# Sparse products by halves of 64 rows on TensorE's column halves, with the gathers of y for eight blocks moved into step 1

## The chip, the cores and the metric

The kernel runs on one core of one Trainium2 chip. A core has a matrix engine (TensorE, in the profile PE, its weight loads PEld), a vector engine (DVE), an activation engine (ACT), a general engine (GpSimd, POOL) and a queue engine that issues most transfers (SyncE, SP). The metric is the time of one execution in microseconds on the device. The kernel before has a median of 1310.05 us over 11 runs (1305.77 to 1312.8).

## The reference

A graph of N = 2708 nodes has features x of 256 columns and a matrix adj (2708 x 2708) in which about 0.3% of the entries are not zero. Two layers follow each other; the second has two steps.

```
x1 = layernorm(x + relu(concat(x, adj @ x) @ weight + bias))     # layer 0
R  = (adj + I) / row sums of (adj + I)                           # layer 1
Xf = Xa = x1;  Z = 0
for n in 0, 1:
    A  = top_p_attention(Xa, W1, W2, W3)   # softmax of q k^T, per row the largest up to 0.9, renormalised
    Xf = R @ Xf
    Xa = A @ Xa
    Z += Xf @ U1[n].T + Xa @ U2[n].T
out = layernorm(x1 + layernorm(x1 + Z) * g + b)
```

Everything is float32. R is as sparse as adj, A is dense before the cut and is computed in full.

## The kernel before, in words

Rows come in NB = 22 blocks of 128, the last of 20 rows (EDGE). D = 256. Products by U1 and U2 are made before those with R and A, so that R is applied to two arrays of 256 columns: yf (s = 0), and v (s = 1), which is v + R yf as it comes out of s = 0. Both lie in DRAM as yf_d and v_d, of which a row of 1 KB belongs to a node.

- **Stage 0 and stage 1** (to 285 us): x @ weight, and then for each block m the dense product of adj, read as 704 KB in two loads, with layer 0's norm. While adj's block lies in SBUF, DVE notes which of its columns hold anything (name_columns, L287).
- **Lists.** An output block has 128 rows, and so few entries that no more than 7 x 128 = 896 of the 2708 columns hold one. Lists (L297) makes a list of these columns for each block: DVE takes the largest eight of each segment again and again (take), up to CAP = 160 a segment; end joins the seven segments of a block into one list, by way of DRAM, with seven scatters of POOL. ix holds the list as CC = 7 columns of 128 indices. Blocks 0 to 15 make one list tile, joined at the end of stage 1, and blocks 16 to 21 another, whose rounds lie in step 1's first nine periods and which is joined at t = 8.
- **Step 1** (349 to 725 us): the loop over t = 0 to 21 with six slots g each: transposes and products of A's block t (turn, products: L527, L564), the logits of t + 3 (L507), the exponentials of t + 2 on ACT, the largest and their sum on DVE. In slot (m - 2, 3) adj_gather(m) has POOL fetch the listed rows of adj's block, transposed in DRAM: 7 indirect transfers of 128 rows of 512 bytes (L367) and one addition of the identity (L369). Four and five slots later adj_store writes them to adjc_d. In (20, 2) and (20, 5) POOL gathers y of blocks 0 and 1 (L719).
- **The border.** ya_pair (L662) projects two blocks of step 1's result by U2 into ya, the tile that step 2's products read; ACT copies each pair (L675, L678). Its tile is otherwise free in step 1. Behind the copies ACT has the exponentials and the search of step 2's first blocks (L966, L969), in the order of its queue.
- **Step 2** (786 us on): 24 periods (per) of six slots. A period has the transposes of block per - 2, its products with ya, the logits and exponentials of block per + 2, a search for the cut on ACT (try_act) and on DVE, and r_units(n): n of R's products, L749. A block has CC + 1 = 8 of them: 7 with gathered columns, one for the block's own 128 columns (own_d), all of them 128 x 128 by 128 x 256 in one accumulator. `units` says how many a period has: 16 ahead of the loop, 8 in periods 0 and 1, 18 in each of periods 2 to 9 (the rest of s = 0), none in 10, 16 in each of 11 to 21 (s = 1).
- **y's ring.** yg has room for two blocks. As r_units begins a block, it loads the next: adj's rows come from adjc_d (SyncE), y's by 7 indirect transfers of POOL (y_load), in both s. s = 1's first load waits until the last v is stored (r_out, `m == NB - 1`). From period 13 on the finals (two norms, out) come with each period; their four additions on POOL stand among the gathers.

The order on each engine is that of the program: the loops write it down, and each engine takes its own instructions one after the other. POOL's indirect transfers are issued by POOL itself, so whatever POOL waits for holds back all behind it; a plain transfer waits in SyncE's queue in the same way.

Of the kernel before, what the change touches and what calls it, by code (L numbers as in the profile page):

```python
# [38 lines left out]
CAP = 160  # L39
ML = 16  # L40
CW, CC = 128, 7
# [11 lines left out]
def gnn_two_layer_kernel(ctx: ExitStack, tc: tile.TileContext, N, xT_d, x_d, adj_d, w0_d, b0_d,  # L53
# [31 lines left out]
    assert NB == 3 * KS + 1 and CW == P and CAP % 8 == 0 and N < NB * P  # L85
# [16 lines left out]
    c.part_d = dram.tile([NB, KS, CAP + 1], FP, name="part_d")  # L102
    c.list_ds = [dram.tile([b - a, KS * CAP], I32, name="list_d") for a, b in ((0, ML), (ML, NB))]
    c.adjc_d = dram.tile([NB, CW, CC * P], FP, name="adjc_d")
    c.yf_d = dram.tile([P, NB, D], FP, name="yf_d")
    c.v_d = dram.tile([P, NB, D], FP, name="v_d")
    c.own_d = dram.tile([NB, P, P], FP, name="own_d")
# [12 lines left out]
    NF = 6 * NB + 4  # L120
# [28 lines left out]
def fast_path(ctx, tc, c, flags, fint, xT_d, x_d, w0_d, b0_d, w1_d, w2_d, w3_d, u1_d, u2_d, g_d, b_d):  # L149
# [43 lines left out]
    xT = big.tile([P, DC, N], FP, tag="Y", name="xT")  # L193
# [73 lines left out]
    names = room[:, :NB * (NB - 1)].rearrange("p (m c) -> p m c", c=NB - 1)  # L267
    at = NB * (NB - 1)
    ramp = room[:, at:at + NB]
    some = room[:, at + NB:at + 2 * NB]  # L270
    LROOM = 3 * P + 2 * CAP + 1 + KS * (CAP + 1)
    first_room = room[:, at + 2 * NB:at + 2 * NB + LROOM]
# [6 lines left out]
    ix = small.tile([P, NB, CC], I32, tag="ix", name="ix", bufs=1)  # L279
    nc.gpsimd.iota(ix.rearrange("p m c -> p (m c)"), pattern=[[0, NB * CC]], base=LAST, channel_multiplier=0)  # L280
    for i, (a, b) in enumerate(((0, ML), (ML, NB))):
        nc.gpsimd.dma_start(out=c.list_ds[i][:, :CW * CC].rearrange("m (p c) -> p m c", c=CC), in_=ix[:, a:b, :])
    before_m = small.tile([NB, 1], FP, tag="before_m", name="before_m", bufs=1)
# [3 lines left out]
    def name_columns(m):  # L287
        for h in range(2):
            nc.vector.tensor_reduce(some[:, h * KH:(h + 1) * KH], adj_of[m][h], AX.X, ALU.max,
                                    apply_absolute_value=True)  # L290
        nc.vector.tensor_scalar(some, some, 0.0, None, op0=ALU.not_equal)
        for a, b, o in ((0, m, 0), (m + 1, NB, -1)):
            if a < b:
                nc.vector.scalar_tensor_tensor(names[:, m, a + o:b + o], ramp[:, a:b], -float(m * P * NB),
                                               some[:, a:b], op0=ALU.add, op1=ALU.mult)

    class Lists:  # L297


        def __init__(self, a, b, flag, room):  # L300
            self.a, self.b, self.n, self.flag = a, b, KS * (b - a), flag
# [22 lines left out]
        def end(self):  # L324
# [9 lines left out]
            nc.gpsimd.dma_start(out=c.part_d[a:b].rearrange("m s k -> (m s) k"), in_=self.out[:n])  # L334
            nc.gpsimd.dma_start(out=self.all, in_=c.part_d[a:b])
            run = small.tile([NB, KS], FP, tag="run", name="run", bufs=1)[:b - a]
            to = small.tile([NB, KS], I32, tag="to", name="to", bufs=2)[:b - a]
# [4 lines left out]
            list_d = c.list_ds[a > 0]  # L342
# [5 lines left out]
            nc.gpsimd.dma_start(out=ix[:CW, a:b, :], in_=list_d[:, :CW * CC].rearrange("m (p c) -> p m c", c=CC))  # L348

    adj_rows = adj_d.rearrange("m p k i -> (m p k) i")  # L350
    staged = {}

    to_turn = []

    def name_y():
        while to_turn:
            m = to_turn.pop()
            nc.gpsimd.tensor_scalar(ix[:CW, m, :], ix[:CW, m, :], m * P * NB, P * NB - 1, op0=ALU.subtract, op1=ALU.min)

    def adj_gather(m):  # L360
# [4 lines left out]
        name_y()  # L365
        for i in range(CC):
            nc.gpsimd.indirect_dma_start(out=a[:CW, i, :], out_offset=None, in_=adj_rows,  # L367
                                         in_offset=bass.IndirectOffsetOnAxis(ap=ix[:CW, m, i:i + 1], axis=0))
        nc.gpsimd.tensor_tensor(a[:p, CC, :], a[:p, CC, :], ident[:p], op=ALU.add)  # L369
        to_turn.append(m)  # L370
        staged[m] = a

    def adj_store(m, h):

        i = (CC + 1) // 2
        if h == 0:
            nc.sync.dma_start(out=c.adjc_d[m, :, :i * P], in_=staged[m][:CW, :i, :].rearrange("p c i -> p (c i)"))
            return
        a = staged.pop(m)
        nc.sync.dma_start(out=c.adjc_d[m, :, i * P:], in_=a[:CW, i:CC, :].rearrange("p c i -> p (c i)"))  # L380
        nc.sync.dma_start(out=c.own_d[m, :rows(m), :], in_=a[:rows(m), CC, :])
# [64 lines left out]
    lists = Lists(0, ML, flags[:, NF - 4:NF - 2], first_room)  # L446
    for m in range(NB):
# [18 lines left out]
        if m == ML:  # L466
            lists.turn()
# [15 lines left out]
        if m >= ML:  # L483
            i = m - ML
            lists.take(CAP // 8 * i // (NB - ML), CAP // 8 * (i + 1) // (NB - ML))
    assert not weights
    lists.end()
    y_room = big.tile([P, DC * N], FP, tag="Y", name="yg")
    YW = 2 * (CC + 1) * D
    yg = y_room[:, :YW].rearrange("p (s c d) -> p s c d", s=2, d=D)  # L490
    spares = [y_room[:, YW + D * i:YW + D * (i + 1)] for i in range(4)]
    lists = Lists(ML, NB, flags[:, NF - 2:], yg[:, 1].rearrange("p c d -> p (c d)"))
# [218 lines left out]
    arrived, loads, held = {}, {}, {}  # L711
    later = [[], []]
    ready = []

    def y_load(s, m):
        y = yg[:, m % 2]
        rows_d = (c.yf_d, c.v_d)[s].rearrange("p k d -> (p k) d")
        for i in range(CC):
            nc.gpsimd.indirect_dma_start(out=y[:CW, i, :], out_offset=None, in_=rows_d,  # L719
# [177 lines left out]
    for t in range(NB):  # L897
# [6 lines left out]
        for g in range(NG):  # L904
# [16 lines left out]
            if g == 2:  # L921
                if t + 3 < NB:
                    extract1(t + 3)
                if t < 9:
                    lists.take(2 * t + 2, 2 * t + 4)
# [805 lines left out]
```

## Time and profile before

| | |
|---|---|
| median of 11 runs | 1310.05 us (1305.77 to 1312.8) |
| profiled execution | 1310.61 us, span 1308.7 us, mean granted clock 0.979 |
| stage 1, one block | 11.03 us (28 to 271 us in all) |
| step 1, one period | 17.54 us (t loop 349 to 725 us) |
| ya, then ACT's start of step 2 | 725 to 752 us, 752 to 786 us |
| step 2, periods 2 to 8 | 24.16 us each |
| step 2, periods with v and finals (15 to 20) | 25.2 us each |
| one product of R (two records) | 0.433 us |
| one gather by POOL | 0.95 us and 0.30 to the next |

The page gives each engine's busy time, the chain of work that ended last (followed back from the last instruction, each piece to what released it), and groups of instructions by line. In float32 one product is two records on PE. A period's time is read as the distance between the first transposes (L527) of two periods in the chain. The time of an execution is its span and about 2 us around it.

### The profile page before, as it was taken

The page shows a single profiled execution, that of the slowest core. Times are in us where ns is not written, and L with a number is a line of the kernel's source. Part 1 is how long each engine was busy: PE and PEld are TensorE (multiplying, and loading weights), DVE is VectorE, ACT ScalarE, POOL GpSimd, SP SyncE. Part 2 cuts the span into 40 slices and gives each one's busy share as a digit, 9 for nine tenths or more (in the row PEclk, how much of TensorE's full clock was granted, in tenths as well). Part 3 has the DMA queues.
Part 4 walks back from the last instruction along what each step waited for, and adds up shares of the span by engine and source line. Part 5 has one row for each costly group of instructions (what it writes and reads, how often), then busy time and mean ns, then how long its engine had stood idle before and what let it go on. Part 6 is the DMA issues. An engine that isn't in the chain of part 4 may idle for free.

```text
span 1308.7 us, 18883 instructions
## 1 busy us (share of the span) xinstructions
PE 1235.3 (94%) x5764; PEld 892.6 (68%) x5764; DVE 996.3 (76%) x3406; ACT 735.1 (56%) x1337; POOL 635.5 (49%) x594
## 2 busy tenths in 40 slices
PE   8999999979899999999999969999998999999985
PEld 6878877843477777777766647777765776666763
DVE  2445554874999997977761389889889899999996
ACT  2000111025555666656555497888878889989931
POOL 1000000003475442677755077788756768888850
PEclk9999999989999999999999989999998999999997
DMA  7465444523322220233223155656644545655541
GB/s 193 151 189 169 155 141 158 165 67 123 113 73 86 69 69 10 60 95 95 81 74 100 50 161 165 191 166 189 196 105 144 170 131 162 191 157 152 173 106 38
DMA packets 101993, 166.27 MB, mean 127 GB/s; under 512 B 17394, under 2 KB 74358, under 8 KB 101882
## 3 DMA queue, kind: packets, MB, share of 16 engines
q1 hardware_dynamic: 75596, 108.91, 26.1%
q0 software_dynamic: 20544, 51.17, 14.9%
q10 hardware_dynamic: 5742, 4.89, 1.4%
q8 instruction: 48, 0.79, 0.3%
q14 instruction: 63, 0.52, 0.1%
HBM read 130.87 MB, written 34.03 MB: 126 GB/s over the span
## 4 chain that ended last, share of the span: by engine, by line
PE 75%; ACT 16%; DVE 5%; issue 2%; DMA 1%; SPq 0%; ACTq 0%; DVEq 0%
PE acc L564 26%; PE acc L257 16%; PE lg L507 9%; PE misc L749 7%; PE tr L527 6%; ACT e L969 3%; ACT e L844 3%; ACT e L966 3%; PE acc L651 2%; ACT wT L530 2%; PE acc L462 2%; PE misc L426 2%; ACT e L848 2%; PE acc L672 2%; PE misc L699 2%
## 5 line engine op out<-in xcount | busy, mean ns | idle before, releaser
L530 ACT COPY wT<-tr 128x512 f32<-128x512 f32 (+2 forms) x258 | 131.8, 518 | 225.1 <-PE tr L527 223.4
L564 PE MATMUL acc<-ya,wT 128*128 128x256 f32 (+1 forms) x924 | 233.9, 393 | 12.5 <-ACT wT L530 12.1
L564 PE MATMUL acc<-x,wT 128*128 128x256 f32 (+1 forms) x924 | 230.5, 388 | 0.0
L719 POOL DMA_INDIRECT yg<-v_d,ix x154 | 193.4, 1256 | 65.8 <-issue 25.6
L564 PEld LDWEIGHTS acc<-ya,wT 128*128 128x128 f32 (+1 forms) x924 | 170.4, 193 | 67.2 <-ACT wT L530 24.3
L564 PEld LDWEIGHTS acc<-x,wT 128*128 128x128 f32 (+1 forms) x924 | 165.2, 189 | 71.0 <-issue 37.4
L719 POOL DMA_INDIRECT yg<-yf_d,ix x154 | 189.3, 1229 | 48.3 <-issue 24.3
L257 PE MATMUL acc<-y,adj_t 128*128 128x257 f32 (+1 forms) x924 | 208.4, 382 | 0.0
L257 PEld LDWEIGHTS acc<-y,adj_t 128*128 128x128 f32 (+1 forms) x924 | 171.8, 189 | 32.7 <-issue 8.9
L367 POOL DMA_INDIRECT adj_t<-in_adj,ix x154 | 167.6, 1088 | 51.5 <-issue 44.0
L749 PE MATMUL misc<-yg,adj_t 128*128 128x256 f32 (+1 forms) x704 | 180.2, 391 | 5.7 <-DMA yg<-yf_d,ix 4.2
L507 PE MATMUL lg<-k,q 64*128 64x512 f32 (+3 forms) x528 | 150.1, 596 | 19.5 <-ACT e L848 12.3
L749 PEld LDWEIGHTS misc<-yg,adj_t 128*128 128x128 f32 (+1 forms) x704 | 125.0, 190 | 53.6 <-issue 22.6
L527 PE MATMUL tr<-ident,e 128*128 128x128 f32 (+2 forms) x946 | 147.4, 275 | 2.3 <-DVE e L1088 2.3
L527 PEld LDWEIGHTS tr<-ident,e 128*128 128x128 f32 (+2 forms) x946 | 113.8, 139 | 41.3 <-issue 18.0
L334 POOL DMA_DIRECT2D part_d<-e x1 | 0.6, 573 | 287.3 <-DVE e L333 287.3
L966 ACT ACTIVATE e<-e,st 128x2708 f32<-128x2708 f32 (+1 forms) x43 | 113.5, 2640 | 0.1
L439 ACT COPY x1T<-tr 128x256 f32<-128x256 f32 (+1 forms) x22 | 8.0, 364 | 186.6 <-PE tr L438 186.6
L969 ACT ACTIVATE e<-e,st 128x2708 f32<-128x2708 f32 (+1 forms) x42 | 110.9, 2642 | 0.1
L570 DVE MAX8 cand<-e 128x8 f32<-128x170 f32 (+1 forms) x352 | 87.2, 318 | 26.8 <-ACT e L514 26.8
L1030 DVE MAX8 cand<-w 128x8 f32<-128x136 f32 (+1 forms) x440 | 106.8, 289 | 0.0
L507 PEld LDWEIGHTS lg<-k,q 64*128 64x128 f32 (+1 forms) x528 | 38.9, 181 | 52.9 <-issue 21.4
(237 smaller groups left out, 1764.6 us busy)
## 6 DMA issues: line engine op xcount, KB each, us to landing
adj_t<-in_adj SPq DMA_DIRECT2D x44, 704.0 KB
adj_t<-adjc_d SPq DMA_DIRECT2D x44, 448.0 KB
adjc_d<-adj_t SPq DMA_DIRECT2D x22, 256.0 KB
base<-za_d SPq DMA_DIRECT2D x41, 128.0 KB
adjc_d<-adj_t SPq DMA_DIRECT2D x22, 192.0 KB
xt<-in_x ACTq DMA_DIRECT2D x21, 128.0 KB
x_d<-x SPq DMA_DIRECT2D x21, 128.0 KB
x1b_d<-xb SPq DMA_DIRECT2D x21, 128.0 KB
```

The source lines that it names most:

```text
L257: nc.tensor.matmul(acc[:p, :n], lhsT=halves[k // KH][:kw, k % KH, :p], rhs=y[:kw, k, :n], start=k == 0, stop=stop and k == NB - 1)
L367: nc.gpsimd.indirect_dma_start(out=a[:CW, i, :], out_offset=None, in_=adj_rows, in_offset=bass.IndirectOffsetOnAxis(ap=ix[:CW, m, i:i + 1] ...
L507: nc.tensor.matmul(lg[:p, h, :b - a], lhsT=q[o, t * P:t * P + p], rhs=keys[s][o, i, :b - a], start=True, stop=True)
L527: nc.tensor.transpose(tr[:kw, k % 4, :p], e[:p, k * P:k * P + kw], ident[:p, :p])
L530: nc.scalar.copy(wT[:, :full, :p], tr[:, :full, :p])
L564: nc.tensor.matmul(acc[:p, :D], lhsT=wT[:kw, k % 4, :p], rhs=y[:kw, k, :], start=k == 0, stop=k == NB - 1)
L570: nc.vector.max(dst[:p, i * 8:(i + 1) * 8], src[:p, i * step:i * step + w])
L719: nc.gpsimd.indirect_dma_start(out=y[:CW, i, :], out_offset=None, in_=rows_d, in_offset=bass.IndirectOffsetOnAxis(ap=ix[:CW, m, i:i + 1], ...
L749: nc.tensor.matmul(acc[:p, :D], lhsT=a[:kw, k, :p], rhs=y[:kw, k, :], start=k == 0, stop=k == CC)
L966: nc.scalar.activation(scr[:b.p, :N], e, AF.Relu, bias=b.nz, scale=b.l[k], accum_out=b.relu)
L969: nc.scalar.activation(scr[:b.p, :N], e, AF.Sign, bias=b.nz, scale=b.l[k], accum_out=b.sign)
L1030: nc.vector.max(b.cand[:p, 8 * i:8 * i + 8], low[:p, SEG2 * i:SEG2 * (i + 1)])
```

## The change

- **Lists by halves.** Every block of 128 rows becomes two halves of HP = 64 rows with a list of its own: CC = 4 columns of 128 indices for each half (NQ = 8 for a block), CAP = 96. An entry of adj_rows is now 64 elements, 256 bytes. ixa, a second index tile, holds the indices of adj's halves, and ix those of y; both are made once per join (columns) rather than per block (name_y goes).
- **Three joins.** Blocks 0 to 8 are joined in stage 1 (m = 19), 9 to 17 in the prologue of step 1, 18 to 21 in step 1 at t = 7, g = 2.
- **The gathers.** adj_gather has 8 transfers (4 for the edge block) for 7; adj_store follows 8 and 9 slots later rather than 4 and 5. y_load has 8 for 7.
- **The products.** For each k of 4, two products of 64 columns of weights stand one after the other, the one on PSUM rows 0 to 63 and the other on rows 64 to 127; then the own product as before. A unit of r_units is a pair or the own product, 5 a block for 8.
- **y ahead.** For blocks 6, 8, ..., 20 and s = 0, POOL gathers y in step 1, in slot (m - 1, 4), into one of two stages that lie in ya's tile (ya[0:8] and ya[8:16]); SyncE stores them nine slots later to yg_d, 1 MB each, and step 2 loads them from there with one transfer of SyncE.
- **The units.** 10 ahead of the loop, 5 in periods 0 and 1, 90 over periods 2 to 8, 5 in the second half of period 9, 105 over periods 10 to 21.

```diff
-CAP = 160
-ML = 16
-CW, CC = 128, 7
+CAP = 96
+LISTS = ((0, 9), (9, 18), (18, 22))
+HP = 64
+AHEAD = tuple(range(6, 22, 2))
+CW, CC = 128, 4
+NQ = 2 * CC
...
+            lists.turn()
+        if m == LISTS[1][1]:
+            first, lists = lists, Lists(1, rooms[1])
             lists.turn()
...
+        if m == LISTS[1][1]:
+            first.end(nc.gpsimd)
+            first.gather(nc.gpsimd)
+        if m == LISTS[1][1] + 1:
+            first.join(nc.gpsimd)
+            first.columns()
...
+        def columns(self):
+            a, b = self.a, self.b
+            for g in range(2):
+                nc.gpsimd.tensor_scalar(ixa[:CW, a + g:b:2, :], ix[:CW, a + g:b:2, :], 2, g, op0=ALU.mult, op1=ALU.add)
+            for m in range(a // 2, b // 2):
+                own = ix[:CW, 2 * m:2 * m + 2, :]
+                nc.gpsimd.tensor_scalar(own, own, m * P * NB, P * NB - 1, op0=ALU.subtract, op1=ALU.min)
...
+    def parts(m):
+        return [(k, g, 2 * k + g) for k in range(CC) for g in range(2 if rows(m) > HP else 1)]
...
+        flat = a.rearrange("p k i -> p (k i)")
+        for k, g, i in parts(m):
+            nc.gpsimd.indirect_dma_start(out=flat[:CW, HP * i:HP * (i + 1)], out_offset=None, in_=adj_rows,
+                                         in_offset=bass.IndirectOffsetOnAxis(ap=ixa[:CW, 2 * m + g, k:k + 1], axis=0))
         nc.gpsimd.tensor_tensor(a[:p, CC, :], a[:p, CC, :], ident[:p], op=ALU.add)
-        to_turn.append(m)
         staged[m] = a
...
+    def y_gather(s, m, y):
+        rows_d = (c.yf_d, c.v_d)[s].rearrange("p k d -> (p k) d")
+        for k, g, i in parts(m):
+            nc.gpsimd.indirect_dma_start(out=y[:CW, i, :], out_offset=None, in_=rows_d,
+                                         in_offset=bass.IndirectOffsetOnAxis(ap=ix[:CW, 2 * m + g, k:k + 1], axis=0))
+
+    def y_stage(m):
+        k = NQ * (AHEAD.index(m) % 2)
+        return ya[:, k:k + NQ, :]
+
+    def y_store(m):
+        nc.sync.dma_start(out=c.yg_d[AHEAD.index(m)], in_=y_stage(m)[:CW].rearrange("p c d -> p (c d)"))
+
     def y_load(s, m):
         y = yg[:, m % 2]
-        rows_d = (c.yf_d, c.v_d)[s].rearrange("p k d -> (p k) d")
-        for i in range(CC):
-            nc.gpsimd.indirect_dma_start(out=y[:CW, i, :], out_offset=None, in_=rows_d,
-                                         in_offset=bass.IndirectOffsetOnAxis(ap=ix[:CW, m, i:i + 1], axis=0))
+        if s == 0 and m in AHEAD:
+            nc.sync.dma_start(out=y[:CW, :NQ, :].rearrange("p c d -> p (c d)"), in_=c.yg_d[AHEAD.index(m)])
+        else:
+            y_gather(s, m, y)
         y_in[s, m] = y
...
-            kw = CW if k < CC else p
-            nc.tensor.matmul(acc[:p, :D], lhsT=a[:kw, k, :p], rhs=y[:kw, k, :], start=k == 0, stop=k == CC)
+            if k < CC:
+                flat = a.rearrange("p k i -> p (k i)")
+                for g in range(2 if p > HP else 1):
+                    w, i = min(p, HP), 2 * k + g
+                    nc.tensor.matmul(acc[HP * g:HP * g + w, :D], lhsT=flat[:CW, HP * i:HP * i + w],
+                                     rhs=y[:CW, i, :], start=k == 0, stop=False)
+            else:
+                nc.tensor.matmul(acc[:p, :D], lhsT=a[:p, CC, :p], rhs=y[:p, NQ, :], start=False, stop=True)
...
+    second.join(nc.gpsimd)
+    second.columns()
...
+    y_ahead = {(m - 1, 4): m for m in AHEAD}
+    y_stores = []
...
-                if t < 9:
-                    lists.take(2 * t + 2, 2 * t + 4)
-                if t == 8:
-                    lists.end()
+                if t < ROUNDS // 2:
+                    lists.take(2 * t, 2 * t + 2)
+                if t == ROUNDS // 2:
+                    lists.end(nc.sync)
+                if t == ROUNDS // 2 + 1:
+                    lists.join(nc.gpsimd)
+                    lists.columns()
+            if (t, g) == (ROUNDS // 2, 5):
+                lists.gather(nc.sync)
             if (t, g) in at:
                 adj_gather(at[t, g])
-                stores += [(NG * t + g + i, at[t, g], i - 4) for i in (4, 5)]
+                stores += [(NG * t + g + 8 + i, at[t, g], i) for i in (0, 1)]
+            if y_stores and y_stores[0][0] <= NG * t + g:
+                y_store(y_stores.pop(0)[1])
+            if (t, g) in y_ahead:
+                m = y_ahead[t, g]
+                y_gather(0, m, y_stage(m))
+                y_stores.append((NG * t + g + 9, m))
...
+    TURN = 9
     units = {0: CC + 1, 1: CC + 1}
     rest = each - first - sum(units.values())
-    units.update({p: rest * (p - 1) // 8 - rest * (p - 2) // 8 for p in range(2, 10)})
-    units.update({p: each * (p - 10) // 11 - each * (p - 11) // 11 for p in range(11, 22)})
+    units.update({p: rest * (p - 1) // (TURN - 2) - rest * (p - 2) // (TURN - 2) for p in range(2, TURN)})
+    units[TURN] = CC + 1
+    rest = each - units[TURN]
+    units.update({p: rest * (p - TURN) // (21 - TURN) - rest * (p - TURN - 1) // (21 - TURN)
+                  for p in range(TURN + 1, 22)})
+
+    def r_share(per, g):
+        late = NG // 2 if per == TURN else 0
+        upto = [units.get(per, 0) * max(0, i - late) // (NG - late) for i in (g, g + 1)]
+        return upto[1] - upto[0]
```

## The prediction

> **What bounds the kernel now.** I read the page's shares, then its chain, then the chain piece by piece through one step-2 period, then windows of one period of each stage, then POOL's and ACT's timelines around the border between step 1 and step 2.
>
> The busy line of PE and the chain:
>
> ```profile
> PE 1235.3 (94%) x5764; PEld 892.6 (68%) x5764; DVE 996.3 (76%) x3406; ACT 735.1 (56%) x1337; POOL 635.5 (49%) x594
> ...
> PE 75%; ACT 16%; DVE 5%; issue 2%; DMA 1%; SPq 0%; ACTq 0%; DVEq 0%
> ```
>
> The chain has PE for 75%, but R's products (L749) are only 7% of it though their group has 180.2 us: most lie beside something else. The second resource is ACT. Windows of one period of step 1, of step 2 with R's first products (s=0), without R, and with R's second products and finals (s=1); the columns are PE, PEld, DVE, ACT, POOL, clock, DMA:
>
> ```profile
> 593.00:610.60 17.60, 17.60 (x90) 12.70 (x88) 13.84 (x54) 10.62 (x21) 12.46 (x13) 1.00 0.34 102
> 841.32:865.50 24.18, 23.87 (x117) 17.99 (x115) 18.71 (x65) 19.93 (x34) 19.38 (x16) 1.00 0.62 180
> 980.90:1004.20 23.30, 19.01 (x79) 12.75 (x78) 20.58 (x77) 19.92 (x33) 13.96 (x13) 0.89 0.43 131
> 1136.30:1161.50 25.20, 23.80 (x112) 16.98 (x111) 23.59 (x86) 22.30 (x40) 20.85 (x19) 1.00 0.56 168
> ```
>
> Step 1 is PE alone. An s=0 period is PE (23.87 of 24.18). The period without R shows what is left without it: ACT's loop. An s=1 period is ACT, with POOL close behind. The chain inside an s=0 period, with PE's work by length:
>
> ```profile
> 936.88 1.13 PE lg L507 x4
> 938.01 1.92 PE acc L564 x8
> 939.93 0.44 PE tr L527 x4
> 940.37 1.30 PE misc L749 x6
> 941.67 1.73 PE acc L564 x8
> ```
>
> A product of R is two of these records: 1.30/3 = 0.433 us. L564's eight records take 1.73 us, but 1.92 behind L507, whose records use half of TensorE's rows: leaving a partial mode costs 0.19.
>
> **The products on column halves.** Before: 44 blocks of 8 products = 3.46 us each. After: 4 pairs of 64-column halves and one full product. How far do a pair's halves overlap? The edge block's last products (L550) stand on four column groups in turn. The chain has them at
>
> ```profile
> 1290.34 3.30 PE acc L550 x44
> ```
>
> that is 75 ns a record where a full one takes 217; the last four run alone (0.86 us), so forty take 2.4 us, 61 ns each, 3.6 of 4 groups at once. I take a pair of halves at the price of one product, 0.433 (bounds: 0.433 and 0.866). But each run of pairs between full-width work changes the mode twice. The edge block's own R products, 20 columns wide, show that (the chain again, 974 us is the neighbour):
>
> ```profile
> 973.01 1.40 PE misc L749 x6
> 974.41 1.92 PE acc L564 x8
> ```
>
> 1.40 for 1.30 and 1.92 for 1.73: 0.10 to enter, 0.19 to leave, 0.3 a run. No skipping it: r_units interleaves two or three units with every transpose and product group.
>
> s=0, periods 2 to 8 (first transposes 788.25 to 957.36, 24.16 each). Before 18 products, 7.79 us. After 90 units over 7 periods, 12.86 each: 10.29 pairs and 2.57 full products, 5.57 us, and about 6.3 runs by 0.3, 1.9 us: 7.46. Some runs follow L507, whose exit is paid anyway (two by 0.1). PE's load falls 0.3 to 0.5. ACT's floor under it: from a period's first transposes to ACT's last wT copy 20.4 us without finals (981.04 to 1001.4), then L564 1.92, and what R has in slot 0: two units and a mode change, 1.2: 23.5. So I take a period of 23.65, a gain of 0.5, and **-3.5** for seven (bounds 0 and -5.5, the latter ACT's floor with two units at no mode price).
>
> The skill has a sterner price. The Trainium skill, "TensorE: Matmul & The Clock Gate", section "Measured speedup vs the span model", gives three column tiles 2.38 times the throughput of one, not 3. No pair of 64 columns runs in this trace, so neither is excluded; by that efficiency a pair would cost some 0.55 us (an estimate), the period 24.7, and this term would be about +3 in place of -3.5.
>
> s=1 and its neighbours. Period 9 now has 5 units in its second half instead of 18: it waits for the first gathers of v, which stand behind the last product of s=0, +1.2 (0 to +3). Period 10 had no units and yet 24.97 us from its first transposes to the next, 1.9 over the following 23.1-23.3, because period 11's first product waited for v; that wait falls into period 9: -1.75. Periods 10 to 21 have 8.75 units for 16; PE is not their bound, ACT's slot 0 carries 1 unit with a mode change (0.73) for 2 (0.87): -0.14 each, and POOL (14 gathers by 1.25 = 17.5, stalls 4.6, four adds by 0.73 = 25.0 of 25.2) allows hardly more. Together **-2** (bounds +2 and -5).
>
> **POOL in step 1.** This is where the change adds most. POOL's timeline of before at the border:
>
> ```profile
> 709.48 0.95 POOL L719 DMA_INDIRECT yg<-yf_d,ix  x1 [0.30 <-issue]
> 710.73 0.95 POOL L719 DMA_INDIRECT yg<-yf_d,ix  x1 [0.30 <-issue]
> 711.98 0.95 POOL L719 DMA_INDIRECT yg<-yf_d,ix  x1 [0.30 <-issue]
> 751.69 0.11 POOL L957 MEMSET e<- 128x12 f32 x1 [38.77 <-PE acc L672]
> ```
>
> A gather takes 1.25 us, whatever the size of its rows (512 bytes of adj at 1.25, 1 KB of y at 1.25): halving adj's rows halves nothing. POOL now ends 39 us before step 2. After: third list joined one period earlier, so free about 505-514 (before 531.8; the seven scatters take 508.3 to 530.8). Until y of block 20 stand 100 gathers of adj and 56 of y: 156 by 1.25 = 195 us, 13 additions of 0.47 = 6, and the stalls: while DVE runs L635 (3.03 us) a gather takes 3.0-3.2, 2.0 to 2.6 more, once a period, 20 to 30 in all. Sum 726 to 746, I take 740. Then it lands (3.3) and SyncE stores 1 MB (3.4 to 5.8 us at the 308 to 180 GB/s of the windows, with 2 or 3 to land): 749.
>
> Who waits: the stage is ya itself, 16 of 22 blocks' room. ya_pair's copy of blocks 8 and 9 overwrites block 20's stage. ACT's timeline of before has that copy, the end of ya, and the exponentials behind it:
>
> ```profile
> 737.38 0.59 ACT L675 COPY ya<-acc 128x512 f32<-128x512 f32 x1 [2.24 <-PE acc L672]
> ...
> 751.60 0.62 ACT L678 COPY ya<-acc 128x256 f32<-128x256 f32 x2 [1.25 <-PE acc L672]
> 752.13 2.65 ACT L966 ACTIVATE e<-e,st 128x2708 f32<-128x2708 f32 x1
> ```
>
> From 752 to 782 the chain is ACT almost alone, in order, so the whole wait at 737.4 reaches the end: 749 - 737.4 = **+11** (0 if the early sum holds, +18 for the late one). While ACT waits, PE stops behind its accumulators and DVE behind L844's results; neither shortens what follows.
>
> y of blocks 0 and 1 comes after that, by 765 or so (before 713), and the gathers of 2 and 3 behind them: **+1** in periods 0 and 1 (0 to +3), whose 5 units for 8 lie beside ACT's chain and save nothing.
>
> SyncE: y_store stands in its queue before za_d's and adj's stores, and waits for POOL, some 15 us late. za's two buffers hold one period each, 35 us, just enough; I cost it nothing, with +5 as upper end. The eight 1 MB loads in step 2 take the place of 64 gathers on POOL, one block in nine us: nothing (0 to +2).
>
> The prologue: list 0 of step 1 goes, list 1 is joined there; its scatters sit on room that ACT's copies need, 0 to +1, hidden by 3 us of slack; and DVE's rounds for lists lose length, where PE is the bound. Nothing. The tail from 1237 is unchanged.
>
> **Sum.** +11 +1 -3.5 -2 = +6.5 on the profiled execution's 1310.61 (span 1308.7 and 1.9 around it), which lies 0.56 above the median of 1310.05: 1316.6 against that median.
>
> **Rivals.**
> 1. Faster: POOL is in time. If DVE's stalls shrink (L635 at 2.0 by ten) and the join is early, block 20 is stored by 738, ACT's wait is 0 and the gains stand alone: 1310.05 - 5.5 + 1 = 1306. For it: POOL's 39 idle us and the early join. Against: 156 gathers cannot take less than 195. It decides at storage before about 739.
> 2. The wait is worse: own-block loads hold POOL (10 waits, 61.9 us in all, at L369 now) or SyncE's queue closes on itself. Each 10 us on POOL there is 10 at the end: 1322 to 1334.
> 3. The halves don't overlap. A pair at 0.866 makes s=0 periods 28.1, +4 by 7, and s=1 PE-bound at about 25.6: 1310 + 28 + 12 + 5 = 1355. Against: L550.
> 4. The change does its work on PE and nothing else moves: as PE's saving is 44 by (3.46 - 2.17) = 57 us of busy time less mode changes of some 25, but ACT's floor is lower than I take it, s=0 gains 1 a period more and s=1 0.5: 1304.
>
> **How the numbers follow.** Forecast (ACT waits 5 to 18 us) 0.55, 1309 to 1324; rival 1 0.17; rival 2 0.18; rival 3 0.03; rival 4 0.07. A measurement can tell 0.2%, 2.6 us. Faster (under 1307.4): most of rivals 1 and 4, 0.22; within: the low end of the forecast and the rest of those, 0.14; slower 0.64. The range leaves out the far half of rivals 2 and 4 and all of 3: 1303 to 1332.
>
> **What would show it.** ACT idle before the ya copy of block 8 for 5 to 18 us, put down to a DMA from yg_d's store; POOL without gaps from 510 to 750. s=0 first transposes 23.5 to 23.9 apart; records of L749 in pairs some ns apart, with 0.3 us of gaps around each run. Wrong it would be if that copy waits for nothing, if s=0 periods shrink to 23 or below, or if step 1's periods (17.54) grow.

## The result, and the profile after

The changed kernel takes 1343.63 us (median, 1339.84 to 1347.65), the kernel before 1311.07 over all its runs by then: a ratio of 1.0255, 95% interval 1.0237 to 1.0272. The forecast was 1316.6 (1303 to 1332): the sign was right, the size was not. The profiled execution's span is 1342.7 us. The runs of this document come in seven sets, each with the kernel before beside it; in four of them that kernel took 1357 to 1370 us instead of 1311 and every version of the changed kernel 1487 to 1551, so from these four disturbed sets only lengths of stages that agree with the other sets are used, and whole times only beside the kernel before of the same set.

Shares and chain on the page of the changed kernel:

```profile
PE 1221.3 (91%) x5839; PEld 823.2 (61%) x5839; DVE 992.5 (74%) x3404; ACT 738.3 (55%) x1342; POOL 687.1 (51%) x663
...
PE 67%; ACT 16%; DMA 6%; DVE 5%; issue 4%; POOL 2%; ACTq 0%; POOLq 0%; DVEq 0%
PE acc L603 23%; PE acc L263 15%; PE lg L546 7%; PE tr L566 6%; PE misc L805 3%; ACT e L1042 3%; ACT e L1039 3%; ACT e L904 3%; DMA xT<-in_xT 2%; PE acc L690 2%; DMA yg<-yf_d,ix 2%; ACT wT L569 2%; PE acc L490 2%; DMA yg<-v_d,ix 2%; PE misc L453 2%
```

PE is busy 14 us less than before, and R's products have gone from 7% of the chain to 4% (L805, and L808 for the own products). But transfers now have 6% of the chain where they had 1%, and one of their names, xT, belongs to stage 0, of which the prediction said nothing.

One period of step 1, two of s = 0 (periods 4 and 5), one of s = 1, in windows (PE, PEld, DVE, ACT, POOL, clock, DMA):

```profile
621.04:638.58 17.54, 17.54 (x91) 12.70 (x89) 13.79 (x53) 10.58 (x21) 13.88 (x13) 1.00 0.43 135
869.10:892.90 23.80, 23.20 (x126) 14.60 (x125) 21.46 (x79) 19.96 (x33) 12.38 (x11) 1.00 0.74 231
892.90:917.70 24.80, 23.71 (x128) 14.31 (x126) 22.18 (x78) 19.96 (x33) 16.38 (x14) 1.00 0.67 205
1185.30:1209.90 24.60, 21.72 (x113) 13.38 (x111) 21.41 (x76) 21.86 (x38) 20.62 (x18) 1.00 0.52 150
```

Step 1's period has not changed. The first s = 0 period is 0.4 us shorter, the second 0.6 longer; PE has 2 us less to do in s = 1.

Lengths of the stages, read as the distance between the starts of their last (or first) products and transposes in each trace; the last two columns are experiments told below:

| us | before | after | own_view_2 | all_three_3 |
|---|---|---|---|---|
| stage 0 | 26.7 | 53.4 | 33.4 | 26.1 |
| stage 1 | 255.5 | 254.9 | 255.3 | 256.2 |
| to step 1's first product | 66.8 | 68.7 | 68.2 | 66.8 |
| step 1 | 376.3 | 374.8 | 377.5 | 376.3 |
| ya | 25.7 | 25.7 | 25.7 | 25.7 |
| to period 2's first transposes | 36.9 | 38.4 | 36.2 | 36.3 |
| period 2 | 24.1 | 29.3 | 31.7 | 24.0 |
| periods 3 to 8 | 145.0 | 143.7 | 143.6 | 143.6 |
| period 9 to the last product | 336.1 | 339.6 | 338.2 | 338.1 |
| the rest | 15.5 | 14.2 | 14.0 | 14.3 |

So 26.7 of the 34.0 us of span are lost in stage 0 and 6.7 between ya and period 3; periods 3 to 8 gain 1.3, and 2.2 are lost behind them. The chain of stage 0, after:

```profile
0.74 3.23 DMA xT<-in_xT
...
3.98 3.32 DMA xT<-in_xT
...
7.32 11.25 DMA xT<-in_xT
...
18.59 6.67 DMA xT<-in_xT
...
25.27 3.64 DMA xT<-in_xT
...
28.93 3.64 DMA xT<-in_xT
...
32.71 21.09 PE misc L419 x86
```

and before:

```profile
3.31 14.66 DMA xT<-in_xT
...
18.98 8.16 PE misc L392 x36
```

SyncE's issues of the seven loads, before and after:

```profile
0.75 3.64 SPq L196 DMA_DIRECT2D xT<-in_xT  x7
```

```profile
0.74 32.22 SPq L202 DMA_DIRECT2D xT<-in_xT  x7
```

Before, SyncE issues all seven loads of xT at once, and PE works on the first blocks while the others land. After, each load waits for the one ahead of it, and PE's second product waits for all seven.

### The profile page after: what moved, and what is told of

It is laid out like the page before. It is cut to its first block, busy times and chain, and to the rows that moved or that the text cites. A ratio compares the mean times of both kernels' runs of the same rounds, so it can differ in the third digit from the quotient of the medians.

```text
span 1342.7 us, 19115 instructions
## 1 busy us (share of the span) xinstructions
PE 1221.3 (91%) x5839; PEld 823.2 (61%) x5839; DVE 992.5 (74%) x3404; ACT 738.3 (55%) x1342; POOL 687.1 (51%) x663
## 4 chain that ended last, share of the span: by engine, by line
PE 67%; ACT 16%; DMA 6%; DVE 5%; issue 4%; POOL 2%; ACTq 0%; POOLq 0%; DVEq 0%
PE acc L603 23%; PE acc L263 15%; PE lg L546 7%; PE tr L566 6%; PE misc L805 3%; ACT e L1042 3%; ACT e L1039 3%; ACT e L904 3%; DMA xT<-in_xT 2%; PE acc L690 2%; DMA yg<-yf_d,ix 2%; ACT wT L569 2%; PE acc L490 2%; DMA yg<-v_d,ix 2%; PE misc L453 2%
## 5 line engine op out<-in xcount | busy, mean ns | idle before, releaser
L757 POOL DMA_INDIRECT yg<-v_d,ix x172 | 220.0, 1279 | 74.4 <-issue 56.3
L603 PE MATMUL acc<-ya,wT 128*128 128x256 f32 (+1 forms) x924 | 236.6, 396 | 21.8 <-ACT wT L569 21.1
L603 PE MATMUL acc<-x,wT 128*128 128x256 f32 (+1 forms) x924 | 230.5, 388 | 0.0
L603 PEld LDWEIGHTS acc<-ya,wT 128*128 128x128 f32 (+1 forms) x924 | 166.6, 192 | 91.7 <-ACT wT L569 40.4
L396 POOL DMA_INDIRECT adj_t<-in_adj,ixa x172 | 182.1, 1059 | 60.2 <-issue 47.4
L603 PEld LDWEIGHTS acc<-x,wT 128*128 128x128 f32 (+1 forms) x924 | 165.2, 189 | 71.0 <-issue 37.4
L757 POOL DMA_INDIRECT yg<-yf_d,ix x108 | 129.3, 1197 | 84.9 <-PE misc L805 59.2
L805 PE MATMUL misc<-yg,adj_t 128*64 128x256 f32 (+1 forms) x688 | 120.0, 410 | 22.5 <-DMA yg<-yf_d,ix 12.4
L805 PEld LDWEIGHTS misc<-yg,adj_t 128*64 128x64 f32 (+1 forms) x688 | 44.2, 138 | 89.1 <-issue 33.4
L757 POOL DMA_INDIRECT ya<-yf_d,ix x64 | 72.6, 1134 | 18.3 <-issue 17.9
```

The source lines that it names most:

```text
L396: nc.gpsimd.indirect_dma_start(out=flat[:CW, HP * i:HP * (i + 1)], out_offset=None, in_=adj_rows, in_offset=bass.IndirectOffsetOnAxis(ap=i ...
L603: nc.tensor.matmul(acc[:p, :D], lhsT=wT[:kw, k % 4, :p], rhs=y[:kw, k, :], start=k == 0, stop=k == NB - 1)
L805: nc.tensor.matmul(acc[HP * g:HP * g + w, :D], lhsT=flat[:CW, HP * i:HP * i + w], rhs=y[:CW, i, :], start=k == 0, stop=False)
```

## The experiments

**Stage 0: is it the view of xT?** The changed kernel has a longer tile and cuts xT out of it. own_view, and own_view_2 with the same program, make it a tile of three dimensions again; before_flat_xT puts the changed kernel's tile into the kernel before.

```diff
-    xT = big.tile([P, YT], FP, tag="Y", name="xT")[:, :DC * N].rearrange("p (c n) -> p c n", n=N)
+    xT = big.tile([P, DC, YT // DC], FP, tag="Y", name="xT")[:, :, :N]
```

> The changed kernel, but xT is a tile of three dimensions again, [128, 2, 2816], of which the first 2708 columns are used; nothing else differs. Theory 1: the 26.7 us of stage 0 come from seven loads of xT that wait for one another (and products that wait for all seven), since the cut-out view of a longer flat tile makes them look as if they overlapped. Then the last product of stage 0 ends near 27 us rather than 53 and the time is 1343.6 - 26.7 = 1317. Rival: the loads are slow by themselves, with the longer pitch of the rows in SBUF: the pitch stays, stage 0 still ends near 53 us, 1343. Second rival: later stages give back part of it (something downstream was covered by the delay): 1320 to 1335.

> own_view once more, on another chip: on the first one the kernel before itself took 1370 us, and step 1 stood for waits that no run elsewhere shows. Theory 1 (the false waits in stage 0): 1317 where the kernel before takes 1311, stage 0 ending near 27 us. Rival: the changed kernel without its delay in stage 0 brings its gathers in step 1 into stalls by itself: step 1 is longer than 376 us here too, and the time is above 1340.

> The kernel before, with only the tile of xT made as in the changed kernel (flat, 5632 long, first 5416 cut out and folded; yg's tile as long). Theory 1: stage 0 ends 26.7 us later, all else the same: 1311 + 26.7 = 1338. Rival (it takes the rest of the change, the third list's transfers on POOL or the smaller loads): 1311.

own_view came in a disturbed set (1546.18 us beside 1369.92). own_view_2: 1324.98, the kernel before beside it 1312.36, ratio 1.0093 (1.0079 to 1.0107); against the changed kernel's +32.6 us that is +12.6. before_flat_xT, in the same set as own_view: 1390.43 beside 1369.92, ratio 1.0158 (1.0099 to 1.0216), +20.5. Its step 1 is disturbed too (402 us), so the stage is the surer figure: stage 0 takes 48.3 us, 21.6 more than in the kernel before. SyncE's timeline of it starts with

```profile
0.75 26.57 SPq L197 DMA_DIRECT2D xT<-in_xT  x7
```

seven issues in 26.6 us where the kernel before needs 3.64. Taken out, the one line gives back 20.0 us of stage 0; put in, it costs 21.6. The rows of xT are as far apart in own_view as in the changed kernel, so it is not the pitch. It is the waits. A load of `[:, :, a:b]` touches two stretches whose starts lie 2708 elements apart; taken for one stretch from the first to the last, it overlaps with the next load's. That the folded view of a longer flat tile is taken so is inferred, as no run shows how the waits are made from the view, but the trace fits it: PE's first product, which reads only the first columns of the first stretch, starts at 4.32 us, and the second, which reads from the other stretch, at 32.71. Theory 1's figure, that all 26.7 us come back, did not hold: stage 0 still takes 33.4 us.

**Stage 0: the other 6.7.** Windows of own_view_2 while xT lands (the last two columns are DMA share and GB/s):

```profile
12.00:15.00 3.00, 3.00 (x16) 2.66 (x15) 0.57 (x2) 0.74 (x2) 0.00 (x0) 1.00 1.06 27
15.00:18.00 3.00, 2.40 (x12) 1.76 (x10) 0.70 (x2) 0.37 (x1) 0.00 (x0) 1.00 1.10 65
18.00:21.00 3.00, 0.30 (x2) 0.31 (x3) 0.00 (x0) 0.00 (x0) 0.00 (x0) 1.00 1.07 124
```

All DMA engines are busy and move 27 to 124 GB/s: small pieces (theory 3). They are the first filling of the lists, issued by POOL in the first microseconds, in 2816 pieces of 28 bytes before and 5632 of 16 after. All of it is one constant, so its layout is free; list_rows, and list_rows_2 with the same program, write it in 176 pieces of 512 bytes.

```diff
-        nc.gpsimd.dma_start(out=c.list_ds[i][:, :CW * CC].rearrange("m (p c) -> p m c", c=CC),
-                            in_=ix[:, 2 * a:2 * b, :])
+        for k in range(CC):
+            nc.gpsimd.dma_start(out=c.list_ds[i][:, P * k:P * (k + 1)],
+                                in_=ix.rearrange("p m c -> p (m c)")[:2 * (b - a), :P])
```

> own_view, and the three lists in DRAM are filled at the start by rows of 512 bytes (176 packets in all) instead of 5632 pieces of 16 bytes (before: 2816 of 28). Theory 3: what stage 0 still loses after own_view (33.4 us for 26.7) is DMA time that these small pieces take from the loads of xT, between 9 and 24 us in the trace: stage 0 ends at 26 to 27 us, 1325 - 6.7 = 1318. Rival: the loss is the longer pitch of xT's rows: 33 us and 1325 as before.

> list_rows once more: theory 3 (the small pieces of the lists' first filling hold back xT) says 1325.0 - 7 = 1318; its rival (the rows' pitch) 1325.

Both came in disturbed sets (1527.63 and 1520.57 us); stage 0 took 26.1 and 26.0 us in their traces, where own_view's took 33.1 and own_view_2's 33.4. Theory 3 holds to the microsecond. Part of its 7 us is not waiting: in own_view_2 PE's last 36 records of stage 0 take 10.58 us, where they took 8.16 before, at a granted clock of 0.55, 0.50 and 0.81 in the windows of 3 us from 21 to 30. all_three_3, which has the same filling, shows the engines' load gone (again DMA share and GB/s at the end):

```profile
12.00:15.00 3.00, 3.00 (x15) 2.65 (x14) 0.61 (x2) 0.74 (x2) 0.00 (x0) 1.00 1.03 416
15.00:18.00 3.00, 3.00 (x15) 2.64 (x14) 0.85 (x2) 0.57 (x2) 0.00 (x0) 1.00 0.98 353
18.00:21.00 3.00, 3.00 (x15) 2.61 (x15) 0.85 (x2) 0.55 (x2) 0.00 (x0) 1.00 0.12 30
```

**The start of step 2.** In the changed kernel's chain, PE waits there for gathers, one after another:

```profile
806.53 2.76 DMA yg<-yf_d,ix
...
812.14 2.75 DMA yg<-yf_d,ix
...
817.16 2.70 DMA yg<-yf_d,ix
...
823.85 7.74 DMA yg<-yf_d,ix
```

Two theories: POOL comes late out of step 1, where it stands 30 us for the third list (join_spread spreads that list's scatters over t = 8 to 12, its load to t = 13 and its arithmetic to t = 15), or the gathers of the blocks ahead of block 6 are too slow for period 2 by themselves (ahead_odd, and no_ahead the other way).

```diff
-                if t == ROUNDS // 2 + 1:
-                    lists.join(nc.gpsimd)
-                    lists.columns()
+                if t == ROUNDS // 2 + 1:
+                    lists.begin_join()
...
+    scatters = [(8, 3), (9, 3), (9, 4), (10, 3), (11, 3), (11, 4), (12, 3)]
...
-AHEAD = tuple(range(6, 22, 2))
+AHEAD = tuple(range(5, 21, 2))
```

> As own_view, and the third list's seven scatters no longer stand in a row on POOL at t = 7: each stands between two bursts of gathers in t = 8 to 12, the load of ix follows at t = 13 on SyncE and the index arithmetic at t = 15. POOL then does not stand for some 30 us (503.7 to 534.0 in the changed kernel) and is done with step 1's gathers some 20 us earlier. Theory 2: the 5.2 us that step 2's start loses (R's products of blocks 2 to 5 wait for gathers that POOL makes late) are POOL's lateness: 1317 - 4 = 1313, with the distance between the first transposes of periods 2 and 3 back from 29.3 to about 25. Rival: that wait is the gathers' own rate (40 gathers by 1.25 us between the border and period 3), however early POOL starts: 1317.

> join_spread once more, beside own_view_2. Theory 2 (step 2's start waits because POOL is late): 4 us less than own_view_2, 1313, and 25 us between the first transposes of periods 2 and 3 for 29.3. Rival (the gathers' own rate): as own_view_2.

> own_view, and y is gathered ahead for blocks 5, 7, ..., 19 rather than 6, 8, ..., 20. Theory 4: the 7.6 us that period 2 loses are the gathers of block 5: its slot in the ring comes free with block 3's last product at the end of period 1, its 8 gathers take 10 us and a landing of 3.5, and period 2's 13 units want it after 9. With block 5 ahead that wait goes: 31.7 us between the first transposes of periods 2 and 3 become 24 to 25, 1325 - 7 = 1318. Rival: blocks 2 to 4 are late too, because POOL still gathers for step 1 until the border: 28 to 30, 1322.

> As own_view, and no y is gathered in step 1 but that of blocks 0 and 1 (AHEAD is empty). Theory: the 64 gathers go to step 2, whose s = 0 periods then need 2.57 blocks by 8 gathers by 1.25 us = 25.7 and 4.6 of stalls, 30.3 us of POOL instead of 24.1 of PE: 7 x 6.2 = +43, less the 5 us that the start loses now: about 1355. Rival: POOL is hidden in step 2 as well, and only the start's 5 us go: 1312.

join_spread_2: 1323.36, ratio 1.0083 (1.0068 to 1.0098), 1.6 us less than own_view_2, whose interval overlaps with that; period 2 takes 29.8 us for 31.7, where theory 2 expected 4 us less in all and a period of 25. (join_spread itself, 1533.64 in a disturbed set, tells nothing more.) POOL does come earlier: it begins with y of block 0 at 723.4 us, in own_view_2 at 738.0. But it begins with block 2 at 762.8 and 762.4, since block 2's place in the ring comes free only as R's first products run, and blocks 2 to 5 then take it 48 us in one row in both. So lateness is the smaller part, and POOL's own pace for these four blocks the larger.

ahead_odd takes block 5 out of that row. It came in a disturbed set (1551.30); its period 2 takes 24.6 us in the trace, as theory 4 said. But so did own_view's in such a set (24.0), where step 1 is so long that POOL is early; alone, then, ahead_odd is not proven, and the sum below is what counts. no_ahead (one execution, 1487.29, in a disturbed set): periods 3 to 7 take 33.4, 34.4, 35.1, 33.6 and 33.5 us where own_view in the same set has 23.7 to 24.8. Without the gathers in step 1, s = 0 is some 3 us a period slower even than the 30.3 that POOL's gathers add up to. Gathering ahead is what makes 13 units a period possible at all.

**The sum.** all_three is own_view, list_rows, join_spread and ahead_odd in one.

> own_view, list_rows, ahead_odd and join_spread together. If the causes add: 1325 - 6.7 - 7 - 1.6 = 1310, some 2 us under the kernel before on the same chip (1312.4). If blocks 2 to 4 are late too: 1313 to 1314. What is left of the change's own gain would be the s = 0 periods (1.4 us there so far), against 2.1 lost from period 9 on.

> all_three once more, on another chip than the one on which step 1 stands for waits that the kernel before has little of. If the causes add (stage 0 back to 26.7 us or less, periods 2 to 3 at 24 to 25): 1310 to 1311 where own_view_2 took 1325.0 and the kernel before 1312.4. Rival: the gathers of blocks 2 to 4 are late without block 5's too: 1313 to 1317.

> all_three, for its whole time where step 1 has no such waits (own_view_2: 1325.0 for 1312.4 before). From the stages that the traces of the other chip show undisturbed (stage 0 at 26 us for 33.4, 25 to 27 us from period 2's to period 3's first transposes for 31.7): 1325 - 7 - 6 = 1312, as the kernel before. Rival: block 2 to 4's gathers stay late where POOL works without pauses: 1316 to 1318.

The first two came in disturbed sets (1516.05 and 1508.95). all_three_3: 1308.36 (1305.83 to 1310.77), the kernel before beside it 1310.75: ratio 0.9982, interval 0.9969 to 0.9995. That is the best version of these runs, 35 us under the changed kernel and 2.4 us, or 0.2%, under the kernel before. Its stages are in the table: stage 0 and period 2 are back, periods 3 to 8 keep their 1.4 us, and the last two stretches together are 0.8 longer.

**Why the halves bring so little: the mode changes.** full_columns does each pair as one product of 128 columns with the first half's y; half of the gathered products are left out.

> all_three, and each pair of 64-column products is one product of 128 columns with the first half's y: half of the gathered products are left out, PE's time per unit stays 0.433 us, and no mode changes are left but L546's. Theory 5 of the prediction (0.3 us for each run of pairs, 6 a period, which the s = 0 periods pay in full): s = 0 periods 23.3 for 23.9, -0.6 by 7 = -4 and -1 after period 9: 1305. Rival: the changes lie beside ACT's loop or behind DVE's r_out, and the periods stay: all_three's time within 1 us.

> full_columns once more (each pair of 64-column products is one of 128 columns; half of the gathered products are left out). Theory 5 (a run of pairs costs 0.3 us of mode changes, and the periods pay for it): s = 0 periods of 23.3 for 23.8, s = 1 periods shorter by 0.3: 5 to 6 us less than all_three_2. Rival: hidden, within 1 us of it.

> full_columns (each pair of 64-column products as one of 128 columns; half of the gathered products are left out), for its whole time beside all_three_3's 1308.4. From its periods on the other chip (23.3 for 23.8 in s = 0, 0.3 less in s = 1): -5, 1303, where period 3 comes as early as in all_three_3. Rival: 1308.

All three came in disturbed sets (1514.99, 1504.74 and 1499.15 us), but their s = 0 periods agree: 23.3, 23.3, 24.4, 24.5, 23.3 and 22.5 us, where all_three_3 has 23.7, 23.8, 24.8, 24.7, 23.9 and 22.6; the six take 141.2 to 141.3 for 143.6 to 144.1 in the three runs of all_three. So theory 5 holds for s = 0, where the mode changes cost 0.1 to 0.6 us a period on the path, 2.3 to 2.9 in all. In s = 1 it does not: six of its periods are 0.2 to 0.3 us shorter (24.27 for 24.57), but period 14 takes 26.0 for 25.5 and period 18 27.3 for 25.5, and periods 11 to 21 together take 266.7 to 267.0 for 266.0. Nor are the mode changes all that holds s = 0 back: without them its six periods are 3.8 us shorter than before, while PE's work is shorter by some 13 (5.57 for 7.79 us a period in the prediction's count). The place of the mode changes in the changed kernel's chain, one s = 0 period:

```profile
880.89 1.01 PE misc L805 x8
881.91 1.92 PE acc L603 x8
...
888.48 1.45 PE misc L805 x12
889.93 1.93 PE acc L603 x8
```

Two pairs (eight records) take 1.01 and three 1.45: 0.44 us for a pair more, so the halves do overlap wholly, with 0.14 to enter here, and L603 has 1.92 for the 1.73 that it takes behind full-width work. In full_columns_3, where R's products are full-width, A's (L615 there) have 1.73 between them:

```profile
1051.85 0.70 PE misc L816 x2
1052.55 1.73 PE acc L615 x8
1054.28 0.86 PE misc L816 x4
```

**Fewer runs of pairs, and slot 0.** slot0_free keeps R out of slot 0 from period 10 on; grouped (its edit is shown) has the same products in fewer, longer runs.

```diff
+        slots = (0, 2, 4, 5) if per < TURN else (3, 4, 5) if per == TURN else (2, 4, 5)
+        if g not in slots:
+            return 0
+        n, i = units.get(per, 0), slots.index(g)
+        return n * (i + 1) // len(slots) - n * i // len(slots)
```

> all_three, and from period 10 on R's units stand in slots 1 to 5 alone; s = 0 is unchanged. The prediction's floor (a period without finals is 22.4 us and what R has in slot 0, as PE there stands in line between the transposes and ACT's copies) says: 0.7 us off each period from 10 to 21, 338 to 331 us from period 9 on, 1308.4 - 7 = 1301. Rival: POOL (14 gathers, stalls and the finals' additions, 25.0 us by the prediction's count) or DVE hold the periods where they are: 1308.

> slot0_free, and the units stand in four slots of a period of s = 0 (0, 2, 4, 5) and in three of s = 1 (2, 4, 5): as many products in fewer runs. Theory 5 (0.3 us for each run): two runs fewer in s = 0 are 0.6 us of PE a period, 7 x 0.5 = -3.5 against slot0_free, and nothing in s = 1: 1297.5. Rival: the longer runs put the next transposes off, and ACT's copies behind them: equal to slot0_free or 2 to 4 us more.

Both came in a disturbed set (1502.76 and 1518.84). slot0_free: periods 11 to 14 take 23.2, 23.3, 23.8 and 24.3 us where all_three_3 has 23.6, 24.1, 24.6 and 25.5: 0.4 to 1.1 less, so R's product in slot 0 is on the path there, as the prediction counted it. But period 16 takes 27.9 for 24.6 and period 20 25.7 for 21.0, and the sum of periods 11 to 21 is 267 for 266. Windows of periods 13, 15 and 16 (PE, PEld, DVE, ACT, POOL):

```profile
1247.70:1271.50 23.80, 21.68 (x112) 13.43 (x111) 22.36 (x77) 21.80 (x38) 19.71 (x18) 1.00 0.52 153
1295.80:1320.50 24.70, 22.53 (x112) 13.89 (x111) 24.09 (x86) 22.29 (x39) 20.73 (x18) 1.00 0.50 148
1320.50:1348.40 27.90, 25.08 (x112) 15.16 (x111) 23.78 (x91) 22.00 (x38) 22.76 (x20) 0.94 0.51 152
```

DVE is busy for 24.09 of 24.70 us in the second, so with R out of ACT's way DVE is next there. The third is another matter: the chain from 1310 to 1351 us is DVE's but for one addition of POOL, yet it holds a gap of DVE of 3.91 us for which the trace shows no wait, and that gap is more than the 3.3 us by which period 16 is longer. What made it was not found. grouped: periods 3 to 8 take 25.5, 28.2, 29.9, 26.1, 25.1 and 24.9 us, 159.5 in all for slot0_free's 144. The traced execution took 1524.38 us, the others 1498.85 to 1540.45 (slot0_free: 1491.52 to 1511.26); how long these periods are in the others was not seen. As far as it goes, the rival was right and too mild. The chain shows the long run, and the transposes and ACT's copy behind it:

```profile
1020.92 1.52 PE misc L817 x12
1022.44 0.60 PE tr L578 x4
...
1023.12 0.58 ACT wT L581
```

How much of the 15 us comes from that, and how much from elsewhere, such as blocks that come in bursts for the ring of two, was not told apart.

**POOL's pace in s = 1.** v_by_sync takes s = 1's odd blocks from yg_d without POOL; its rows are s = 0's, not v's.

```diff
-        if s == 0 and m in AHEAD:
+        if m in AHEAD:
```

> all_three, and in s = 1 the odd blocks 5 to 19 take their y from yg_d by one transfer of SyncE, as in s = 0: 64 gathers fewer on POOL, and s = 1's products get s = 0's rows, which are not v's. Theory 6 (from period 9 on POOL's 172 gathers set the pace: four periods of 25.5 to 26.7 among 24.6): the stretch from period 9 to the last product of A falls from 338 to about 332, no period above 25. Rival: ACT's loop sets it, 337 to 338.

It came in a disturbed set (1508.61). Its periods 11 to 17 are 23.6, 24.1, 24.6, 25.1, 25.1, 24.6 and 24.6, where all_three_3 has 23.6, 24.1, 24.6, 25.5, 25.0, 24.6 and 24.6. With 64 gathers fewer, s = 1 is the same but for some tenths: periods 11 to 21 take 263.9 us for 266.0, a third of the 6 us that theory 6 expected. POOL does not set the pace of most periods there; theory 6 is out as the main cause.

## Why the prediction was wrong, and where it was right

Step by step, in us of the profiled executions:

| step of the prediction | said | measured |
|---|---|---|
| stage 0 | not named | +26.7 |
| stage 1, prologue, step 1 | 0 | -0.3 |
| ACT's copy of ya waits for block 20 | +11 | 0 |
| periods 0 and 1 | +1 | +1.5 |
| s = 0, periods 2 to 8 | -3.5 | +3.9 (period 2 +5.2, periods 3 to 8 -1.3) |
| period 9 to the end | -2 | +2.2 |

Without stage 0 the terms add up to +7.3 us, close to the +6.5 of the prediction's sum. That is luck: of the terms behind stage 0 only the smallest came out near what was said.

- **The step that failed is one that the prediction does not have.** It went through what the change says it does, step 1, its prologue, the border and step 2, and left stage 0 at nothing without a reason. The new tile of xT, two lines of the change, is not in it. The view in those lines makes seven loads wait for one another (20 us), and the finer lists double the small pieces of their first filling (7 us). What could have shown the first is a list of what each transfer of SyncE waits for, held against that of the kernel before, for all of the kernel and not for the part that the change is about. None of the rivals had it: 1343.63 lies between rival 2's 1334 and rival 3's 1355, and neither of the two happened.
- **ACT's wait for block 20's store: mechanism right, size wrong.** POOL's gathers for block 20 end, SyncE stores them, and ACT's copy of blocks 8 and 9 starts, at

```profile
756.97 0.95 POOL L757 DMA_INDIRECT ya<-yf_d,ix  x1 [0.31 <-issue]
758.22 0.95 POOL L757 DMA_INDIRECT yg<-yf_d,ix  x1 [0.30 <-issue]
```

```profile
760.01 0.32 SPq L765 DMA_DIRECT2D yg_d<-ya  x1
```

```profile
765.19 0.59 ACT L714 COPY ya<-acc 128x512 f32<-128x512 f32 x1 [3.68 <-DMA yg<-yf_d,ix]
```

  The view names a gather as what ACT waited for, but one of the semaphores that this copy waits for is the store's, and its last count comes at 764.94, after the pair's products on PE (761.71 to 763.70); so the wait is the one that the prediction named. Less the 27.9 us by which step 1 is late, the gathers end at 730.0, inside the 726 to 746 of the working, but I took 740; landing and store took 7.3 us, not 9. The copy idles 3.68 us instead of 2.24, and ya as a whole ends no later. The term was the difference of two large numbers, and I took a middle where the lower end meant nothing.
- **The gathers of blocks 2 to 5 were left out of period 2.** The prediction asked when blocks 0 and 1 come and allowed 1 us, at most 3, in periods 0 and 1 for the two behind them; these cost 1.5. It did not follow blocks 4 and 5. In the changed kernel POOL gathers y of blocks 0 to 5 in one row until 830 us, and period 2, which begins at 816 and needs blocks 4 and 5, is 5.2 us longer. join_spread shows that POOL's lateness out of step 1 is the smaller part of that, and all_three_3 that with block 5 gathered ahead as well period 2 is back at 24.0.
- **The halves' price was right.** A pair takes 0.44 us (said 0.433), 0.14 to enter a mode (said 0.10) and 0.19 to leave it. The Trainium skill, "TensorE: Matmul & The Clock Gate", section "Measured speedup vs the span model", has 2.38 for three tiles of 32 columns; the pairs of 64 columns here do not show that loss, and the measurement decides. Two of the working's side figures do not follow from their parts, though nothing rested on them: a period of 24.7 would have made the term +3.8, not about +3, and ACT's floor with two units at no mode price is 23.19, which makes its lower bound -6.8, not -5.5.
- **The path of s = 0 was half right.** The first two whole s = 0 periods, 23.74 and 23.85, are the 23.65 of the working within 0.2. But the next two are 24.78 and 24.69, and that was not foreseen. The chain there is ACT's from 893.5 on, and then:

```profile
909.14 0.15 DVE bulk L912
909.30 0.84 DVE w L1156
...
910.51 2.98 DVE e L1161 x2
...
913.62 0.50 DVE base L836
...
914.16 0.65 PE misc L805 x4
```

  R's next products wait for the accumulator that DVE's r_out (L836) reads and so frees, and that stands behind DVE's mask of 2.98 us. Over periods 3 to 8 PE's share of the chain goes from 87% to 61%, and ACT and DVE take most of the rest. A likely reason, not tested, is that with 2.6 blocks a period in place of 2.25 PE catches up with DVE: the next wait behind the one that goes.
- **Period 9 to the end.** Period 9 lost 1.3 (said 1.2) and period 10 gained 1.2 (said 1.75); the fault lies behind them. Periods 16 and 17 are 24.62 for 25.2, more than was said, but periods 11 to 13 are 0.3 to 0.8 longer, period 18 takes 26.7 for 25.2 and period 21 25.9 for 23.1: 4.5 us more over periods 11 to 21, of which 2.4 come back in period 22 and the tail. POOL's number of gathers does not explain most of that (v_by_sync), and what does stays open: slot0_free points at DVE in one period, but in the changed kernel itself that was not tried.

## What to carry to other kernels

Hold the waits of every queue against the kernel before over the whole program, not only around the change: a longer tile and a folded view of it can put one transfer behind another far from what was edited. Where work is moved off a late engine, ask who is next in its queue as well as who waits at the border. And a saving on the busiest engine counts only up to the next wait, here ACT's loop, DVE's release of an accumulator, and the mode changes that the smaller products bring with them.

## What the runs showed of the hardware that was not expected

- 5632 pieces of 16 bytes took all DMA engines for some 15 us (9 to 24 us in own_view_2), at 27 to 128 GB/s where all_three_3, without them, moves 353 to 416 until its loads have landed; they cost 7 us of stage 0.
- In the four disturbed sets step 1 of the changed kernel's versions took 474 to 590 us instead of 376, and 402 in the kernel before with the flat tile. The border behind it is 8 to 14 us longer, and periods 9 and 10 together 7 to 15. The instructions are the same; PE's records are somewhat longer (L603 with x 417 ns on the mean in own_view, 388 in own_view_2), ACT's are not. The chain of own_view there has

```profile
413.13 22.94 another core or an unknown queue
```

  PE's transposes had started by 413.1; the trace has PE's next increments of the semaphore that ACT waits for at 414.87 and 436.08. POOL issued gathers back to back until 432.6. Such waits make 130 us of own_view's chain up to 950 us, 76 of no_ahead's and 14 of before_flat_xT's, in the order of the gathers that each has in step 1, though not in proportion to them; that the gathers cause them is not shown. The expectations took the chip for the difference, but own_view and own_view_2, one program, have the same chip number on record. Why increments come late in these sets, and not in own_view_2, stays open.
